# Target rows of a graph layer: a gather per edge replaced by one-hot matmuls on TensorE

## The chip, the core and the metric

The kernel runs on one core of a Trainium2 chip. The metric is the device time of one launch in microseconds (us), as the median of several runs without the profiler; lower is better. PE is TensorE, DVE is VectorE, ACT is ScalarE, POOL is GpSimd and SP is SyncE.

## The reference, cut to what matters

3125 nodes of 512 features and 50000 edges go through one layer with three parts: a message-passing network, a linear attention and a mixture of eight experts. The change concerns the messages. Per edge (`edge_dst` is the graph's `src`, which is sorted into target tiles by the kernel itself; `edge_src` its `dst`):

```python
pre = irrep_linear(x, W_pre0, b_pre0, W_pre1)
p0, p1 = split_irreps(pre)
pd0 = p0[edge_dst]
ip1 = jnp.einsum('eum,eum->eu', p1[edge_dst], p1[edge_src]) / 3.0
s0 = jnp.concatenate([pd0, pd0, ip1], axis=-1)
...
w = ssp(edge_attr @ W_f1) @ W_f2 * (ssp(s0 @ W_s1) @ W_s2)
w1, w2, w3, w4 = jnp.split(w, 4, axis=-1)
x0e, x1e = split_irreps(x[edge_src])
...
out = jax.ops.segment_sum(edge_feat, edge_dst, num_segments=old_x.shape[0])
```

So an edge needs two rows of its target (p0 folded into 32 hidden values, and p1, 384 values) and two of its source (p1 again, and the 512 values that make the message). `edge_feat` is made of `w`, the source's values and four edge numbers `sh`; the messages are summed per target.

## The kernel before, in words

The kernel has four stages. First, edges are sorted by target on the chip and their records (48 numbers) are scattered to memory in that order, while the node rows are computed; the rows go to two tables in memory, `rows_d` (target part, 32 + 384 values) and `rows_s` (source part, 384 + 512). Second comes the edge stage, from line 779, with which the change deals. Then the sums become new node rows and are routed, and last the experts run.

A target tile is 125 nodes, held as two halves of 63 and 62 (`TG`, `HT` = 64 rows of a half). A tile of edges is 128 edges whose targets lie in one half. Two edge tiles, one for each half, are a pair; eight pairs make up a target tile (`PER`), 25 target tiles make 200 pairs, and 12 more pairs (`NOV_MOST`) take what is over. Two pairs, four edge tiles, are a quad (`G`), with one record tile `rec`. The 212 pairs are 106 quads.

The order on PE, ACT, DVE and POOL is written out by hand (`tc.manual_schedule`, line 989): each engine runs its instructions in the order of the program text, and SP's transfers are put in order by the framework. A loop over steps `s` issues, in each step, the work of several pairs at different stages, and some of it only for a quad, every second step (`due`):

- `load` (SP): the record of a quad, 14 pairs ahead; `clear` (DVE) blanks places not in use, 10 ahead.
- `fetch` (POOL), `LEAD` = 9 pairs ahead: per edge tile one indirect transfer of the target rows `gd` (line 825) and one of the source rows `gx` (line 829).
- `products` (DVE, line 840), 7 or 6 pairs ahead: target p1 times source p1, into `prod`.
- `turn` (PE, line 847) 5 ahead: twelve transposes that also add the three components, into PSUM tile `ps_ip`; `turn2` copies it out on ACT (line 855).
- `hidden` (PE, lines 861, 866, 871), 4 ahead: the 32 hidden values of four tiles in one PSUM tile `ps_h`: the edge's own values turned, the target's values turned, and the inner products times `W_s1`.
- `softplus` (ACT, from line 879) and `softplus2` (DVE, line 891), 3 and 2 ahead; `which` (DVE, line 898): a one-hot of the edge's place in its half, 128 × 64 for each tile; `scaled` (ACT, line 913): the one-hot times each of the four edge numbers.
- `weigh`, 1 ahead: PE makes `wa` and `wb` (lines 924, 928), ACT copies `wa` to `wt` (line 930), DVE multiplies `wt` by `wb` (line 931).
- `feats` (DVE, lines 945, 949), 1 ahead: the message features `ft`.
- `gather_up` (PE, line 969): one-hots times features, summed in PSUM tile `ps_s` over the eight pairs; `kept` copies the sum to `acc`.

In a step of the kernel before, DVE runs clear, softplus2, which, products, then the multiplication of `weigh`, then `feats`. PE runs the weights, the hidden layer or the transposes, then the gather-up.

PSUM tiles before: `ps_ip` and `ps_h` one buffer each, `wa` and `wb` one each of 2 × 512 values, `ps_s` two.

Of the kernel before, what the change touches and what calls it, by code (L numbers as in the profile page):

```python
# [16 lines left out]
P = 128  # L17
EDGES = 50000
TG = 125
# [29 lines left out]
def gnn_mix_moe_kernel(ctx: ExitStack, tc: tile.TileContext, a: dict, out: bass.AP):  # L49
# [54 lines left out]

    rows_d = dram.tile([N, HID + 3 * MUL], F32, name="rows_d")
    rows_s = dram.tile([N, 3 * MUL + D], F32, name="rows_s")
# [33 lines left out]
    with ExitStack() as c1:  # L140
# [27 lines left out]
        for r in range(4):  # L168
# [5 lines left out]

        zero = tmp.tile([P, G * REC], F32, name="zero")
        nc.vector.memset(zero, 0.0)
        by_quad = recs.rearrange("(q p i) f -> p q (i f)", p=P, i=G)
        per = PER // PR
        cleared = [
            nc.gpsimd.dma_start(by_quad[:, qs, :], zero.unsqueeze(1).to_broadcast([P, n, G * REC]))  # L180
            for qs, n in (
                (slice(per - 1, NFIX // PR, per), NG), (slice(NFIX // PR, (NFIX + NOV_MOST) // PR), NOV_MOST // PR),
            )
        ]


# [592 lines left out]
    with ExitStack() as c2:  # L779
# [4 lines left out]
        ps_w = c2.enter_context(tc.tile_pool(name="ps_w", bufs=1, space=PSUM, reuse_waits="tile"))  # L784
        ps_o = c2.enter_context(tc.tile_pool(name="ps_o", bufs=2, space=PSUM, reuse_waits="tile"))

        w_s1c = w.tile([P, HID], F32, name="w_s1c")
# [12 lines left out]
        class Quad:  # L800
            pass

        quads = [Quad() for _ in range(NQ)]

# [13 lines left out]
        def fetch(Q, k):  # L818

            if k == 0:  # L820
                Q.gd = gat.tile([P, G, HID + 3 * MUL], F32, name="gd", bufs=3)
                Q.gx = gat.tile([P, G, 3 * MUL + D], F32, name="gx", bufs=5)
            reci = Q.rec.bitcast(I32)
            for i in (2 * k, 2 * k + 1):
                nc.gpsimd.indirect_dma_start(  # L825
                    out=Q.gd[:, (i + 2) % G, :], out_offset=None, in_=rows_d[:, :],
                    in_offset=bass.IndirectOffsetOnAxis(ap=reci[:, i, 5:6], axis=0),
                )
                nc.gpsimd.indirect_dma_start(  # L829
                    out=Q.gx[:, i, :], out_offset=None, in_=rows_s[:, :],  # L830
                    in_offset=bass.IndirectOffsetOnAxis(ap=reci[:, i, 4:5], axis=0),
                )

        def products(Q, k):

            if k == 0:
                Q.prod = work.tile([P, G, 3 * MUL], F32, name="prod")
            x = slice(2 * k, 2 * k + 2)
            d = slice(2 - 2 * k, 4 - 2 * k)
            nc.vector.tensor_mul(Q.prod[:, d, :], Q.gd[:, d, HID:], Q.gx[:, x, : 3 * MUL])  # L840

        def turn(Q):

            ps = ps_a.tile([P, G, P], F32, name="ps_ip")
            for i in range(G):
                for b in range(3):
                    nc.tensor.matmul(  # L847
                        ps[:, i, :], Q.prod[:, i, b * P : (b + 1) * P], ident, is_transpose=True,
                        start=(b == 0), stop=(b == 2),
                    )  # L850
            Q.ps_ip = ps
# [5 lines left out]
        def hidden(Q):  # L857

            Q.ps = ps_a.tile([P, 2, P], F32, name="ps_h")
            for i in range(G):  # L860
# [3 lines left out]
                )  # L864
            for i in range(G):
                nc.tensor.matmul(
                    Q.ps[i * HID : (i + 1) * HID, 1, :], Q.gd[:, i, :HID], ident,
                    start=True, stop=False, tile_position=(0, i * HID),
                )
            for i in range(G):  # L870
# [3 lines left out]
                )  # L874

        def softplus(Q, after=None):

            sp = work.tile([P, P], F32, name="sp")
            nc.scalar.activation(sp, Q.ps[:, 1, :], AF.Abs)
            if after is not None:  # L880
# [5 lines left out]
            Q.sp = sp  # L886
            Q.hT = work.tile([P, 2, P], F32, name="hT")
            nc.scalar.copy(Q.hT[:, 0, :], Q.ps[:, 0, :])

        def softplus2(Q):  # L890
            nc.vector.scalar_tensor_tensor(
                Q.hT[:, 1, :], Q.ps[:, 1, :], 0.0, Q.sp, op0=ALU.max, op1=ALU.add
            )

        def which(Q):

            Q.one = work.tile([P, G, HT], F32, name="one")
            nc.vector.tensor_tensor(
                Q.one, lane[:, :HT].unsqueeze(1).to_broadcast([P, G, HT]),
                Q.rec[:, :, 6:7].to_broadcast([P, G, HT]), op=ALU.is_equal,  # L900
            )

        class Pair:
            def __init__(self, Q, j):
                self.Q, self.j = Q, j
                self.tiles = (2 * j, 2 * j + 1)

        def scaled(R):

# [7 lines left out]
        def weigh(R):  # L917
# [4 lines left out]
            for k, i in enumerate(R.tiles):  # L922
                r = slice(i * HID, (i + 1) * HID)
                nc.tensor.matmul(wa[:, k, :], Q.hT[r, 0, :], w_f2[r, :], start=True, stop=True)  # L924
            for k, i in enumerate(R.tiles):
                i = (i + 2) % G
                r = slice(i * HID, (i + 1) * HID)
                nc.tensor.matmul(wb[:, k, :], Q.hT[r, 1, :], w_s2[r, :], start=True, stop=True)  # L928
            R.wt = work.tile([P, PR, D], F32, name="wt")
# [59 lines left out]
        with tc.manual_schedule(engines=steady):  # L989
# [21 lines left out]
            for s in range(-LEAD - 5, n_pairs + 1):  # L1011
                for Q in due(s + LEAD + 5):
                    q = quads.index(Q)
                    loaded = load(Q, recs[q * G * P : (q + 1) * G * P, :])
                    if q == 0:
                        for put in placed:
                            waits_for(loaded, put)
                for Q in due(s + LEAD + 1):
                    q = quads.index(Q)
                    clear(Q, real_slot[:, PR * q : PR * (q + 1), :])  # L1020
                for R in pair(s + LEAD):
                    fetch(R.Q, R.j)
                for Q in due(s + 2):
                    softplus2(Q)
                for Q in due(s + 3):
                    which(Q)
                for k in range(2):
                    for Q in due(s + 7 - k):
                        products(Q, k)
                for R in pair(s + 1):  # L1030
                    weigh(R)
                kept(s - 1)
                for Q in due(s + 3):
                    softplus(Q, table)
                for Q in due(s + 4):
                    hidden(Q)
                for Q in due(s + 5):
                    turn(Q)
# [6 lines left out]
                for R in pair(s):  # L1045
                    if s >= NFIX or s % PER == 0:
                        sums = ps_o.tile([P, D], F32, name="ps_s")
                    R.ps = sums
# [9 lines left out]
        with tc.If(some > NOV_MOST):  # L1058
            with tc.For_i(NOV_MOST // PR, (some + 1) // PR, 1) as i:
# [7 lines left out]
                clear(Q, real)  # L1067
                for k in range(2):
                    fetch(Q, k)
                for k in range(2):  # L1070
                    products(Q, k)
                turn(Q)
                turn2(Q)
                hidden(Q)
                softplus(Q)
                softplus2(Q)
                which(Q)
                for j in range(PR):
                    R = Pair(Q, j)
                    scaled(R)  # L1080
                    weigh(R)
                    feats(R)
                    ps = ps_o.tile([P, D], F32, name="ps_s")
                    gather_up(R, ps, True, True)
                    keep_sums(tile_of(whose[:, j : j + 1]), ps)

# [462 lines left out]
```

## Time and profile before

| what | us |
|---|---|
| median of three runs without profiler (2767.28 to 2779.3) | 2773.01 |
| the profiled execution's own time | 3138.92 |
| its span | 3137.2 |
| PE busy in the span (81%) | 2525.6 |
| DVE busy (54%) | 1684.5 |
| POOL busy (58%) | 1822.3 |
| ACT busy (37%) | 1162.2 |
| gathers of `gd`, 424 | 445.7 |
| gathers of `gx`, 424 | 483.7 |
| gather-up on PE (L969), 3392 instructions | 588.2 |

The profiled execution is longer than the runs without the profiler, so its own time is the base for sums that use its durations. The page of a profile cuts the span into 40 slices of 78 us and shows the busy share of each engine in tenths:

```profile
PE   2576493882788888888888888888679999999998
DVE  7988330211667777776777767777842222222222
POOL 0688666664656666666666666664345555555552
PEclk9688696995888889888898988889889999999999
```

PEclk is the clock that PE was granted, in tenths of full speed. The edge stage is the even stretch from about the eleventh slice to the twenty-eighth. Line numbers (L825) are those of the kernel before. "A <- B" means that A waited for B, or that A's output is made from B; "issue" is a wait that the profile gives no cause for. A matmul of 32-bit numbers shows as two instructions, so that counts of PE are double there.

### The profile page before, as it was taken

The page shows a single profiled execution, that of the slowest core. Times are in us where ns is not written, and L with a number is a line of the kernel's source. Part 1 is how long each engine was busy: PE and PEld are TensorE (multiplying, and loading weights), DVE is VectorE, ACT ScalarE, POOL GpSimd, SP SyncE. Part 2 cuts the span into 40 slices and gives each one's busy share as a digit, 9 for nine tenths or more (in the row PEclk, how much of TensorE's full clock was granted, in tenths as well). Part 3 has the DMA queues.
Part 4 walks back from the last instruction along what each step waited for, and adds up shares of the span by engine and source line. Part 5 has one row for each costly group of instructions (what it writes and reads, how often), then busy time and mean ns, then how long its engine had stood idle before and what let it go on. Part 6 is the DMA issues. An engine that isn't in the chain of part 4 may idle for free. (4 is left out here: it accounts for less than half of the span.)

```text
span 3137.2 us, 46186 instructions
## 1 busy us (share of the span) xinstructions
PE 2525.6 (81%) x16716; PEld 1592.3 (51%) x16716; DVE 1684.5 (54%) x3084; ACT 1162.2 (37%) x3261; POOL 1822.3 (58%) x1741
## 2 busy tenths in 40 slices
PE   2576493882788888888888888888679999999998
PEld 2343242551333444343444434343568888888887
DVE  7988330211667777776777767777842222222222
ACT  1244240110555555555565555556411111111111
POOL 0688666664656666666666666664345555555552
PEclk9688696995888889888898988889889999999999
DMA  7777202555666667676676766676662442785552
GB/s 257 245 262 247 70 24 91 163 175 162 202 204 207 204 197 221 201 212 200 206 218 207 213 204 201 198 206 146 214 247 66 147 149 68 265 291 171 176 171 103
DMA packets 200361, 581.25 MB, mean 185 GB/s; under 512 B 55130, under 2 KB 80400, under 8 KB 189374
## 3 DMA queue, kind: packets, MB, share of 16 engines
q0 software_dynamic: 126176, 455.15, 46.9%
q1 hardware_dynamic: 50718, 83.23, 7.7%
q10 hardware_dynamic: 23232, 39.84, 4.0%
q8 instruction: 135, 2.21, 0.3%
q14 instruction: 100, 0.82, 0.1%
HBM read 635.69 MB, written 112.28 MB: 238 GB/s over the span
## 5 line engine op out<-in xcount | busy, mean ns | idle before, releaser
L829 POOL DMA_INDIRECT gx<-rows_s,rec x424 | 483.7, 1141 | 262.1 <-DVE ft L949 138.5
L969 PE MATMUL ps_s<-ft,ones 128*64 128x256 f32 (+1 forms) x3392 | 588.2, 481 | 17.8 <-issue 15.2
L825 POOL DMA_INDIRECT gd<-rows_d,rec x424 | 445.7, 1051 | 266.5 <-issue 108.1
L459 POOL DMA_INDIRECT recs<-again,at_i x391 | 425.8, 1089 | 236.0 <-issue 111.6
L931 DVE TENSOR_TENSOR wt<-wt,wb 128x1024 f32<-128x1024 f32 x212 | 258.4, 1219 | 382.4 <-ACT wt L930 236.9
L913 ACT ACTIVATE ones<-one,rec 128x64 f32<-128x64 f32 x1696 | 428.1, 339 | 0.0
L1411 PE MATMUL ps_f<-h,we 128*128 128x128 f32 x3392 | 406.7, 278 | 17.9 <-ACT h L1424 15.2
L969 PEld LDWEIGHTS ps_s<-ft,ones 128*64 128x64 f32 x3392 | 254.8, 149 | 301.5 <-issue 238.0
L1411 PEld LDWEIGHTS ps_f<-h,we 128*128 128x128 f32 x3392 | 388.6, 192 | 32.1 <-ACT h L1424 24.9
L949 DVE TENSOR_TENSOR ft<-wt,gx 128x768 f32<-128x768 f32 x424 | 386.0, 952 | 0.0
L930 ACT COPY wt<-wa 128x1024 f32<-128x1024 f32 x212 | 214.3, 1011 | 424.6 <-PE wb L928 207.0
L1426 DVE TENSOR_SCALAR h<-ps_f,bias 128x128 f32<-128x128 f32 x318 | 108.3, 350 | 482.1 <-PE ps_f L1411 450.7
L1338 POOL DMA_INDIRECT we<-w_rows,w_at x212 | 214.7, 1013 | 259.5 <-PE ps_y L1442 101.0
L1424 ACT ACTIVATE h<-ps_f,bias 128x128 f32<-128x128 f32 x318 | 110.7, 366 | 672.9 <-PE ps_f L1411 607.1
L928 PE MATMUL wb<-w_s,hT 32*128 32x512 f32 x848 | 270.8, 655 | 11.2 <-issue 8.3
L924 PE MATMUL wa<-w_f,hT 32*128 32x512 f32 x848 | 252.9, 650 | 7.5 <-issue 5.7
L840 DVE TENSOR_TENSOR prod<-gd,gx 128x768 f32<-128x768 f32 x212 | 202.3, 954 | 33.9 <-DMA gx<-rows_s,rec 21.5
L1411 PEld LDWEIGHTS ps_f<-xt,we 128*128 128x128 f32 x1696 | 199.2, 193 | 26.0 <-issue 24.9
L847 PEld LDWEIGHTS ps_ip<-ident,prod 128*128 128x128 f32 x1272 | 140.4, 143 | 122.4 <-issue 122.3
L1411 PE MATMUL ps_f<-xt,we 128*128 128x128 f32 x1696 | 199.6, 276 | 0.7 <-ACT xt L1359 0.7
L847 PE MATMUL ps_ip<-ident,prod 128*128 128x128 f32 x1272 | 166.7, 281 | 41.4 <-DVE prod L840 33.5
L1442 PE MATMUL ps_y<-we,h 128*128 128x512 f32 x424 | 196.1, 605 | 0.8 <-ACT h L1424 0.7
(337 smaller groups left out, 3114.0 us busy)
## 6 DMA issues: line engine op xcount, KB each, us to landing
w_rows<-in_Wh ACTq DMA_DIRECT2D x24, 1024.0 KB
rows_s<-r SPq DMA_DIRECT2D x24, 448.0 KB
rec<-recs SPq DMA_DIRECT2D x106, 96.0 KB
lined<-rec SPq DMA_DIRECT2D x14, 672.0 KB
again<-lined POOLq DMA_DIRECT2D x14, 672.0 KB
w_rows<-in_Wo ACTq DMA_DIRECT2D x8, 1024.0 KB
gd<-rows_d,rec POOLq DMA_INDIRECT x424
gx<-rows_s,rec POOLq DMA_INDIRECT x424
```

Of the source, the lines that this page charges most:

```text
L459: put = nc.gpsimd.indirect_dma_start(out=recs[:, :], out_offset=bass.IndirectOffsetOnAxis(ap=at_i[:m, t : t + 1], axis=0), in_=again[c][:m ...
L825: nc.gpsimd.indirect_dma_start(out=Q.gd[:, (i + 2) % G, :], out_offset=None, in_=rows_d[:, :], in_offset=bass.IndirectOffsetOnAxis(ap=reci ...
L829: nc.gpsimd.indirect_dma_start(out=Q.gx[:, i, :], out_offset=None, in_=rows_s[:, :], in_offset=bass.IndirectOffsetOnAxis(ap=reci[:, i, 4:5 ...
L847: nc.tensor.matmul(ps[:, i, :], Q.prod[:, i, b * P : (b + 1) * P], ident, is_transpose=True, start=(b == 0), stop=(b == 2),)
L913: nc.scalar.activation(R.ones[:, k, c, :], R.Q.one[:, i, :], AF.Copy, scale=R.Q.rec[:, i, c : c + 1])
L924: nc.tensor.matmul(wa[:, k, :], Q.hT[r, 0, :], w_f2[r, :], start=True, stop=True)
L928: nc.tensor.matmul(wb[:, k, :], Q.hT[r, 1, :], w_s2[r, :], start=True, stop=True)
L931: nc.vector.tensor_mul(R.wt, R.wt, wb)
L949: nc.vector.tensor_mul(R.ft[:, k, MUL : 7 * MUL].rearrange("p (b c u) -> p b c u", b=2, c=3), w[:, k, :, 1, :].unsqueeze(2).to_broadcast([ ...
L969: nc.tensor.matmul(to, R.ones[:, k, m, :], what, start=(first and m == 0), stop=(last and m == 3), tile_position=(0, k * HT),)
L1338: nc.gpsimd.indirect_dma_start(out=dst, out_offset=None, in_=src, in_offset=bass.IndirectOffsetOnAxis(ap=at[:, j : j + 1], axis=0), bounds ...
L1411: nc.tensor.matmul(pss[f], ws[l][:, k, f * P : (f + 1) * P], h[:, k, :], start=(k == 0), stop=(k == 3))
```

## The change

The target rows of an edge tile are no longer gathered by edge. The rows of a half target tile (64 rows) are loaded once for all eight pairs into a tile `own` by plain transfers on SP (`targets`), and PE spreads them over the edges: the one-hot of an edge tile is turned (`over`: two transposes a quad, copied to `oneT` by ACT), and `own_rows` multiplies it with `own`, so that each edge gets its target's row, in PSUM tile `gd`. `products` reads `gd` there, once a pair. `hidden` takes the target's hidden values from `own` and `oneT` in the same way. `which` moves from 3 pairs ahead to 10 ahead, with six buffers.

`ps_one`, `ps_ip` and `ps_h` share one PSUM buffer (tag "turned"); `ps_s` has one buffer[...]. `hidden2` copies the hidden layer's PSUM tile out on ACT, and the softplus works on the copy.

The order in a step changes too: fetch, weigh, kept, softplus2, products, clear, which, over, softplus, hidden, own_rows, turn, feats, turn2, scaled, gather_up. Two more rows of zeros stand at the end of `rows_d`, so that the last half tile can be loaded whole.

```diff
-    rows_d = dram.tile([N, HID + 3 * MUL], F32, name="rows_d")
+    rows_d = dram.tile([N + 2, HID + 3 * MUL], F32, name="rows_d")
...
+        for part in (slice(0, HID), slice(HID, HID + 3 * MUL)):
+            nc.gpsimd.dma_start(rows_d[N:, part], zero[:2, : part.stop - part.start])
...
-        ps_o = c2.enter_context(tc.tile_pool(name="ps_o", bufs=2, space=PSUM, reuse_waits="tile"))
...
         def fetch(Q, k):
...
             for i in (2 * k, 2 * k + 1):
                 nc.gpsimd.indirect_dma_start(
-                    out=Q.gd[:, (i + 2) % G, :], out_offset=None, in_=rows_d[:, :],
-                    in_offset=bass.IndirectOffsetOnAxis(ap=reci[:, i, 5:6], axis=0),
-                )
-                nc.gpsimd.indirect_dma_start(
                     out=Q.gx[:, i, :], out_offset=None, in_=rows_s[:, :],
...
+        def targets(b):
+            own = gat.tile([P, HID + 3 * MUL], F32, name="own", bufs=4)
+            for k in range(PR):
+                nc.sync.dma_start(own[k * HT : (k + 1) * HT, :], rows_d[bass.ds(b * TG + k * (HT - 1), HT), :])
+            return own
+
+        def which(Q):
+            Q.one = work.tile([P, G, HT], F32, name="one", bufs=6)
...
+        def over(Q):
+            ps = ps_a.tile([P, G, P], F32, name="ps_one", tag="turned")
+            for j in range(PR):
+                nc.tensor.transpose(
+                    ps[:, j, :], Q.one[:, PR * j : PR * (j + 1), :].rearrange("p k t -> p (k t)"), ident
+                )
+            Q.oneT = work.tile([P, PR, P], F32, name="oneT", bufs=4)
+            nc.scalar.copy(Q.oneT, ps[:, :PR, :])
+
+        def own_rows(R):
+            R.gd = ps_a.tile([P, PR, D], F32, name="gd")
+            for k in range(PR):
+                h = slice(k * HT, (k + 1) * HT)
+                nc.tensor.matmul(
+                    R.gd[:, k, : 3 * MUL], R.Q.oneT[h, R.j, :], R.own[h, HID:], start=True, stop=True,
+                    tile_position=(k * HT, 0),
+                )
...
-            nc.vector.tensor_mul(Q.prod[:, d, :], Q.gd[:, d, HID:], Q.gx[:, x, : 3 * MUL])
+            nc.vector.tensor_mul(Q.prod[:, d, :], R.gd[:, :, : 3 * MUL], Q.gx[:, x, : 3 * MUL])
...
             for i in range(G):
+                R = Q.pairs[1 - i // PR]
+                h = slice(i % PR * HT, (i % PR + 1) * HT)
                 nc.tensor.matmul(
-                    Q.ps[i * HID : (i + 1) * HID, 1, :], Q.gd[:, i, :HID], ident,
-                    start=True, stop=False, tile_position=(0, i * HID),
+                    Q.ps[i * HID : (i + 1) * HID, 1, :], R.own[h, :HID], Q.oneT[h, R.j, :],
+                    start=True, stop=False, tile_position=(i % PR * HT, i * HID),
                 )
...
+        def hidden2(Q):
+            Q.hT = work.tile([P, 2, P], F32, name="hT", bufs=3)
+            nc.scalar.copy(Q.hT, Q.ps[:, :2, :])
...
+                for R in pair(s + LEAD + 3):
...
+                        R.own = targets(at // PER)
...
+                for R in pair(s + LEAD):
+                    fetch(R.Q, R.j)
+
+                for R in pair(s + 1):
+                    weigh(R)
+                kept(s - 1)
+                for Q in due(s + 2):
+                    softplus2(Q)
+                for R in pair(s + 7):
+                    products(R)
                 for Q in due(s + LEAD + 1):
                     q = quads.index(Q)
                     clear(Q, real_slot[:, PR * q : PR * (q + 1), :])
-                for R in pair(s + LEAD):
-                    fetch(R.Q, R.j)
-                for Q in due(s + 2):
-                    softplus2(Q)
-                for Q in due(s + 3):
                     which(Q)
-                for k in range(2):
-                    for Q in due(s + 7 - k):
-                        products(Q, k)
-                for R in pair(s + 1):
-                    weigh(R)
-                kept(s - 1)
+                for Q in due(s + LEAD):
+                    over(Q)
                 for Q in due(s + 3):
                     softplus(Q, table)
                 for Q in due(s + 4):
                     hidden(Q)
+                    hidden2(Q)
+                for R in pair(s + 8):
+                    own_rows(R)
                 for Q in due(s + 5):
                     turn(Q)
                 for R in pair(s + 1):
...
                     if s >= NFIX or s % PER == 0:
-                        sums = ps_o.tile([P, D], F32, name="ps_s")
+                        sums = ps_a.tile([P, D], F32, name="ps_s")
```

The branch for more than 12 pairs over is changed alike; with these inputs it is not entered. `weigh` issues the same four matmuls in another order (wa, wb, wa, wb).

## Prediction

> **What bounds the kernel now.** I read the granted clock and the totals first, then busy time by stage, then the timeline of one quad (four edge tiles, two pairs) inside the edge stage, then the waits there. By stage (columns: stretch, length, busy time and count of PE, PE's weight loads, DVE, ACT, POOL, then granted clock, DMA share, GB/s):
>
> ```profile
> 742.70:797.00 54.30, 15.38 (x124) 10.51 (x124) 13.08 (x20) 9.40 (x29) 39.24 (x39) 0.53 0.77 234
> 797.00:2213.60 1416.60, 1209.73 (x8788) 569.34 (x8780) 1028.75 (x1369) 788.04 (x2435) 890.17 (x810) 0.89 0.68 200
> ...
> 2280.00:3137.20 857.20, 818.62 (x5824) 698.54 (x5824) 228.31 (x577) 139.55 (x373) 427.24 (x423) 0.99 0.49 167
> ```
>
> The edge stage is 1416.6 us of 3137.2 us for 106 quads: 13.4 us each. The rest of the profiled time of 3138.9 us is 1722.3 us. The expert stage (from 2280) has PE busy nearly all along; the change doesn't touch it.
>
> The quads are not alike: the transposes L847, one burst per quad, start at 1052.09, 1061.58 and 1079.42 us, 9.49 and then 17.84 us apart. In the short quad the engines look like this (start, duration, engine, line):
>
> ```profile
> 1057.03 1.01 ACT L930 COPY wt<-wa 128x1024 f32<-128x1024 f32 x1 [0.32 <-PE wb L928]
> 1057.08 0.28 DVE L891 SCALAR_TENSOR_TENSOR hT<-ps_h,sp 128x128 f32<-128x128 f32 x1
> 1057.28 0.95 DVE L840 TENSOR_TENSOR prod<-gd,gx 128x768 f32<-128x768 f32 x1
> 1057.41 0.16 PEld L861 LDWEIGHTS ps_h<-ident,rec 128*32 128x32 f32 x8 [1.25 <-DVE rec L813]
> ...
> 1058.14 1.22 DVE L931 TENSOR_TENSOR wt<-wt,wb 128x1024 f32<-128x1024 f32 x1
> ...
> 1058.21 2.37 PE L969 MATMUL ps_s<-ft,ones 128*64 128x512 f32 x16
> ...
> 1060.51 0.70 PE L924 MATMUL wa<-w_f,hT 32*128 32x512 f32 x2
> ...
> 1061.58 1.53 PE L847 MATMUL ps_ip<-ident,prod 128*128 128x128 f32 x12
> ...
> 1063.05 2.37 PE L969 MATMUL ps_s<-ft,ones 128*64 128x512 f32 x16
> ```
>
> From start to next start on PE: hidden layer (L861, 866, 871) 0.80, gather-up (L969) 2.30 per pair, weights (L924/928) 1.07 per pair, transposes 1.46; per quad 0.80 + 2×2.30 + 2×1.07 + 1.46 = 9.0 us with hardly a gap. DVE's ops in the same spacing make 9.7 us: per pair 0.86 (L840) + 1.25 (L931) + 0.61 + 1.74, per quad 0.78 more. POOL's gathers follow each other by 0.95 + 0.30 = 1.25 us at best, eight a quad: 10.0 us; with their mean durations it is 4×(1.05 + 1.14 + 0.60) = 11.2. Three engines sit near 10 us. In the long quads PE issues a few matmuls every 1.4 us and waits for nothing that is named:
>
> ```profile
> PEld ps_s L969 <- issue: 201.9, 630, 1.9
> DVE wt L931 <- ACT wt L930: 187.5, 76, 5.9
> ACT wt L930 <- PE wb L928: 173.2, 95, 4.9
> POOL gx L829 <- DVE ft L949: 116.8, 39, 5.1
> POOL gd L825 <- PE ps_h L866: 84.4, 33, 7.8
> ```
>
> (waiter, releaser, total, times, longest, from 1000 to 2200 us). POOL's own waits are for buffers, so POOL runs ahead. The reader should take two things from it: POOL isn't alone at the limit, and L931 follows ACT's copy, which follows PE, in every pair.
>
> The run without the profiler takes 2773 us, 366 less. The expert stage can't give that; the unnamed PE waits can. I hold them for a cost of profiling, an inference. POOL's floor of 10.0 us lets the edge stage shrink by 1416.6 − 1060 = 357 at most; some of the 366 may sit before 742, where the waits called remote and issue add up to some 156 us (ACT r L709 101.0 and DVE y L734 54.8). Halfway, 80, the edge stage before is 1131 us unprofiled, 10.7 a quad.
>
> [...] after PE's idle from 458.85 to 461.60 (2.75 us) the clock was 0.50 from 463 to 466; after one of 2.37 us at 468 it stayed up. [...] four 32-row matmuls of L924 and L928 start within 0.02 us.
>
> **The change, part by part.**
>
> Removed: 424 gd gathers. POOL falls from eight gathers to four, 5.0 to 5.6 us a quad; the DMA engines lose 424 × 213 KB = 90 of 581 MB and get some 8 MB of direct loads back. Neither was alone at the limit, so this by itself is worth at most 11.2 − 9.7 us a quad, and what is late next are DVE and PE.
>
> Added on ACT: copies of oneT and of two hidden columns of tiles, each 256 wide; between 0.245 (128 wide) and 0.586 (512 wide) that is 0.36 each, less the 0.245 of L888: +0.5 us on 7.4 busy a quad. Covered. DVE: the product reads gd from PSUM instead; L931 reads PSUM at 1.22 us for 1024 and L840 SBUF at 0.95 for 768, the same rate, so 0. SP: `own`, two loads per eight pairs, asked for at pair s+12 and used at s+8, four steps ahead; its queue only holds record loads that wait for `scaled` of pair s−1. Covered; for the last twelve pairs, where each has its own load behind `hidden` of an earlier pair, up to 1.5 us each, not counted. The zero rows and the larger memset stand at the program's start under DVE and POOL work: 0.
>
> Added on PE: `over`, 2 of the 12-transpose kind, 0.24 us a quad; `own_rows`, per pair two matmuls of 384 columns over 64 rows in different row groups: from 1.07 us for 512 columns side by side, 0.80; in series it would be 1.60. The hidden layer's rows of `own` swap one set of four for another: 0. PE's work is then 9.0 + 0.24 + 1.60 = 10.9 us.
>
> The new wait decides. `gd` has one buffer. In step s, own_rows(s+8) overwrites what products(s+7) reads, and products was moved behind weigh(s+1) on DVE, whose L931 waits for ACT's copy, which waits for PE's weights of the same step. Behind own_rows on PE stand the transposes and the gather-up, and behind them the next step's weights. So the step becomes a ring through three engines, once a pair. Walk it from the start of wa at 0: ACT starts at 1.18 (1055.85 to 1057.03) and takes 1.01; DVE starts 0.03 later, 2.22; L931 holds it 1.25, to 3.47; the product 0.95, to 4.42; PE takes the signal 0.05 later, 4.47 (L861 after L891 shows that lag); own_rows to 5.27. Odd step: transposes 1.46, gather-up 2.30: 9.03. Even step: softplus2 is ahead of the product, +0.20; no transposes: 4.67 + 0.80 + 2.30 = 7.77. `over` and the hidden layer fall into PE's wait, so they cost nothing. `turn` needs the shared bank from the oneT copy, done at about 2.6: hidden too. Sum 16.8 us a quad.
>
> PE then idles from 1.4 to 4.5 in the odd step and from 2.0 to 4.7 in the even one: 3.0 and 2.7 us, just the size after which the clock halved above. Bounds: never, 0; always down to a mean of 0.8, then the 9.7 us of PE in the ring cost 9.7 × 0.25 = 2.4. I take about one fall a quad, 3 us at half speed with some two thirds of it on PE work: +1.0. Quad 17.8.
>
> Sum: 106 × 17.8 = 1887; twelve additions of late sums (L977, 0.68) now lie in the ring, +8; the fill from 742.7 to 797 is paced by ten pairs of gathers and loses half, −25. Edge and fill change by 1887 + 8 − 25 − 1416.6 = +453, so 3138.9 becomes about 3592 on the profile's footing. Of the 1722.3 us outside, 80 don't occur without the profiler (0 to 156): 3512. I say 3510, 27% over the median. That the unnamed PE waits vanish in the edge stage needs no subtraction here: the ring replaces that stage.
>
> **The rivals.**
> - The ring isn't closed (gd is free when PE comes, PE only gets more work): quad 10.9 + 0.4 gap (9.49 less PE's 9.07 now) = 11.3, edge 1198, total 1722 + 1198 − 25 − 80 = 2815. For it: PE is the busiest engine. [...]
> - Not slower: POOL paces the unprofiled kernel at 11.2 us a quad, and PE at 10.9 keeps under it. Gain 106 × 0.3 + 25 = 57: 2716. Place: the gather stream; it decides only if PE's stall per quad stays under 0.3 us. Against: a stall of 5.7 is worked out above.
> - The clock stays down at 0.6 in most of the stage: 9.7 × 0.67 = 6.5 more, quad 23.3, edge 2470 + 8: total 1722 + 2478 − 25 − 80 = 4095. For it: every gap is near the size. Against: own_rows, transposes, gather-up and weights are 5 to 6 us of dense work between gaps.
> - own_rows in series: +1.6 a quad, 3680, inside the range.
>
> **How the numbers follow.** Forecast with its own range 0.80, clock down 0.08, ring open 0.07, not slower 0.05. Low end: no fall of the clock and 156 us taken off, 1722.3 − 156 + 1781 + 8 − 25 = 3330, 3325 stated. High end: 2.4 us a quad for the clock and nothing taken off, 1722 + 2035 − 17 = 3740. Half a per cent is about what a measurement of this kernel can tell from no change: faster 0.04, within it 0.02, slower 0.94.
>
> **What would show it.** DVE's product waits for nothing, but PE's own_rows waits for DVE's product some 2.5 to 3 us, twice a quad; L931 again behind ACT's copy; POOL half idle, waiting for feats; quads 17 to 18 us apart; clock in the stage below 0.95; own_rows 0.8 us from start to next start. I am wrong if PE runs through own_rows without a wait, or if the expert stage changes.

## The result, and the profile after

The changed kernel takes 3724.9 us (3722.76 to 3726.74, four runs) against 2773.31 us for the kernel before in the same comparison: a ratio of 1.3431 (95% interval 1.3401 to 1.3461). It is slower by a third. The forecast was 3510 us with a range from 3325 to 3740.

By stage, from the answer that lists stretches of the span (length, busy time and count of PE, PE's weight loads, DVE, ACT and POOL, then granted clock, DMA share, GB/s):

```profile
900.00:2700.00 1800.00, 1332.26 (x8272) 599.48 (x8272) 853.01 (x1143) 710.90 (x2130) 332.68 (x352) 0.79 0.31 98
...
2800.00:3723.00 923.00, 860.23 (x6232) 740.08 (x6232) 305.28 (x743) 191.28 (x455) 454.73 (x474) 0.97 0.52 176
```

No engine is full in the edge stage: PE is busy for 74% of it, DVE for 47%, POOL for 18%, and PE's clock is 0.79. The page's slices show the same over the whole span:

```profile
PE   2667991777777777777777777777776799999998
POOL 0887777211212111211112121212102455555553
PEclk9888995778777777877787777778778899999999
```

The gather-up (now line 997) starts first at 688.3 us and last at 2831.2: the stage has become 2142.9 us long. What lies outside it, 3724.9 − 2142.9 = 1582 us, is what it was before (1584, by the first experiment). So all of the loss is in the edge stage. The waits there (waiter, releaser, total us, times, longest):

```profile
POOL gx L825 <- DVE ft L977: 1593.5, 101, 18.0
ACT wt L958 <- PE wb L956: 826.2, 210, 8.0
DVE wt L959 <- PE ps_h L905: 619.4, 103, 7.5
...
PE gd L860 <- DVE prod L872: 542.0, 203, 6.0
DVE wt L959 <- ACT wt L958: 503.9, 108, 6.2
```

PE waits at `own_rows` (L860) for DVE's product in 203 of 212 pairs. DVE waits at the weights' multiplication (L959, before L931) for ACT in the odd steps. In the even ones the name beside it is the hidden layer, but L959 doesn't read `ps_h`, and it starts 0.03 us after ACT's copy ends in both. ACT waits for PE's weights. Each of the three waits for the one before it in a circle. POOL only waits for a buffer of `gx` to come free.

The timeline of one turn and a half (start, duration, engine, line, tile; in brackets the idle time before it and what ended it):

```profile
1504.21 1.65 PE L860 MATMUL gd<-own,oneT 64*128 64x384 f32 x4 [2.38 <-DVE prod L872]
...
1505.79 4.54 PE L997 MATMUL ps_s<-ft,ones 128*64 128x512 f32 x16
...
1516.35 2.82 PE L879 MATMUL ps_ip<-ident,prod 128*128 128x128 f32 x12
...
1531.51 0.69 PE L955 MATMUL wa<-w_f,hT 32*128 32x512 f32 x1
...
1532.70 1.01 ACT L958 COPY wt<-wa 128x1024 f32<-128x1024 f32 x1 [6.01 <-PE wb L956]
...
1533.74 1.22 DVE L959 TENSOR_TENSOR wt<-wt,wb 128x1024 f32<-128x1024 f32 x1 [4.05 <-ACT wt L958]
...
1534.88 0.95 DVE L872 TENSOR_TENSOR prod<-gd,gx 128x768 f32<-128x768 f32 x1
...
1535.98 0.92 PE L860 MATMUL gd<-own,oneT 64*128 64x384 f32 x4 [2.96 <-DVE prod L872]
...
1536.83 1.53 PE L879 MATMUL ps_ip<-ident,prod 128*128 128x128 f32 x12
...
1538.29 2.37 PE L997 MATMUL ps_s<-ft,ones 128*64 128x512 f32 x16
```

From 1531.51 on this is an odd step at full clock, and it is the predicted ring. Counted from the start of `wa` at 1531.51: ACT starts after 1.19, DVE after 2.23, the product after 3.37, own_rows after 4.47, and the next `wa` (1540.59) after 9.08 us, with 9.03 worked out ahead. The three lines at the top are the same work at half clock: own_rows takes 1.65 instead of 0.92, the gather-up 4.54 instead of 2.37, the transposes 2.82 instead of 1.53. Transposes of successive quads start 20.48 us apart (1495.86, 1516.35, 1536.83). The sum had 17.8.

The granted clock has only two values here, 0.50 and 1.00, and the stretches between its changes, over two quads, are these (columns as in the table by stage, the clock third from the end):

```profile
1503.54:1510.37 6.83, 6.16 (x24) 2.33 (x24) 3.62 (x6) 0.96 (x5) 2.30 (x3) 0.50 0.18 38
1510.37:1513.78 3.41, 1.43 (x10) 0.43 (x10) 1.25 (x2) 2.21 (x5) 1.49 (x2) 1.00 0.90 294
1513.78:1520.61 6.83, 5.84 (x20) 3.48 (x22) 3.18 (x4) 1.40 (x5) 0.00 (x0) 0.50 0.23 86
1520.61:1527.44 6.83, 4.45 (x50) 1.78 (x46) 3.04 (x6) 4.40 (x15) 0.00 (x0) 1.00 0.17 46
1527.44:1530.85 3.41, 3.41 (x14) 1.42 (x14) 2.25 (x3) 0.00 (x0) 0.89 (x1) 0.50 0.00 0
1530.85:1544.50 13.65, 8.98 (x82) 4.17 (x78) 6.10 (x8) 7.36 (x22) 2.90 (x4) 1.00 0.46 143
```

At 1544.50 the next fall begins, 40.96 us after the first one here, and the pattern starts again.

### The profile page after: what moved, and what is told of

Read it like the earlier page. It is cut to its first block, busy times and chain, and to the rows that moved or that the text cites. A ratio compares the mean times of both kernels' runs of the same rounds, so it can differ in the third digit from the quotient of the medians.

```text
span 3723.0 us, 47635 instructions
## 1 busy us (share of the span) xinstructions
PE 2859.6 (77%) x17776; PEld 1719.9 (46%) x17776; DVE 1683.4 (45%) x3084; ACT 1232.4 (33%) x3367; POOL 1291.0 (35%) x1319
## 5 line engine op out<-in xcount | busy, mean ns | idle before, releaser
L825 POOL DMA_INDIRECT gx<-rows_s,rec x424 | 401.2, 946 | 1702.7 <-DVE ft L977 1593.5
L959 DVE TENSOR_TENSOR wt<-wt,wb 128x1024 f32<-128x1024 f32 x212 | 258.9, 1221 | 1127.3 <-PE ps_h L905 619.4
L997 PE MATMUL ps_s<-ft,ones 128*64 128x256 f32 (+1 forms) x3392 | 736.8, 594 | 18.7 <-DVE acc L1005 18.7
L860 PE MATMUL gd<-own,oneT 64*128 64x384 f32 x848 | 277.1, 733 | 561.7 <-DVE prod L872 542.0
L997 PEld LDWEIGHTS ps_s<-ft,ones 128*64 128x64 f32 x3392 | 298.6, 184 | 458.5 <-issue 422.4
L860 PEld LDWEIGHTS gd<-own,oneT 64*128 64x128 f32 x848 | 89.2, 245 | 614.3 <-issue 333.1
L955 PE MATMUL wa<-w_f,hT 32*128 32x512 f32 x848 | 243.1, 646 | 0.0
L956 PE MATMUL wb<-w_s,hT 32*128 32x512 f32 x848 | 242.9, 646 | 0.0
L879 PEld LDWEIGHTS ps_ip<-ident,prod 128*128 128x128 f32 x1272 | 198.1, 183 | 85.8 <-issue 85.3
L879 PE MATMUL ps_ip<-ident,prod 128*128 128x128 f32 x1272 | 232.0, 352 | 0.0
L887 ACT COPY ip<-ps_ip 128x512 f32<-128x512 f32 x106 | 62.1, 586 | 466.2 <-PE ps_ip L879 466.2
```

The costliest lines, as they stand in the source:

```text
L825: nc.gpsimd.indirect_dma_start(out=Q.gx[:, i, :], out_offset=None, in_=rows_s[:, :], in_offset=bass.IndirectOffsetOnAxis(ap=reci[:, i, 4:5 ...
L860: nc.tensor.matmul(R.gd[:, k, : 3 * MUL], R.Q.oneT[h, R.j, :], R.own[h, HID:], start=True, stop=True, tile_position=(k * HT, 0),)
L879: nc.tensor.matmul(ps[:, i, :], Q.prod[:, i, b * P : (b + 1) * P], ident, is_transpose=True, start=(b == 0), stop=(b == 2),)
L956: nc.tensor.matmul(wb[:, k, :], Q.hT[q, 1, :], w_s2[q, :], start=True, stop=True)
L959: nc.vector.tensor_mul(R.wt, R.wt, wb)
L997: nc.tensor.matmul(to, R.ones[:, k, m, :], what, start=(first and m == 0), stop=(last and m == 3), tile_position=(0, k * HT),)
```

## The experiments

Three questions were open: is it the ring, and the ring alone, that holds PE up; how much is the clock's; and what paced the kernel before, on which the worth of the whole change hangs. The runs were made on four chips. On two of them (e0 to e3; e10 and e11) the kernel before takes 2765 to 2769 us, as on the chip of the result above, on the other two (e4 to e7; e8 and e9) 3198 to 3200, so times are compared within one chip, and between the two kinds of chip only by the length of the edge stage (first to last start of the gather-up) or by the distance between quads. The changed kernel's 3724.9 us goes with 2773 us for the kernel before, 0.3% above the 2765 of e0 to e3, and is set beside them.

### The kernel before, profiled again (e0)

The same kernel, to see whether the profiler or something else made the first profile 366 us longer than the median.

> The kernel before, profiled once more. The profile of before took 3139 us against a median of 2773, the profile of the changed kernel 3724.8 against 3724.9. Theory P (profiling slows the kernel before, by PE's unnamed waits): again about 3140, with quads 9.5 and 17.9 us apart. Rival (that execution was an odd one, and profiling costs nothing): 2770 to 2785, quads about 11.2 us apart (2773 less the 1554 us that the changed kernel spends outside 106 quads of 20.48, over 106, is 11.5 with the fill in it).

It took 2759.36 us under the profiler, and the median of nine runs without it on that chip was 2764.84. The profiler costs nothing that can be seen. The edge stage as a stretch, and POOL's timeline in it:

```profile
691.80:1866.90 1175.10, 1024.39 (x8783) 514.18 (x8780) 1032.87 (x1367) 783.26 (x2426) 882.41 (x813) 0.96 0.81 242
```

```profile
1205.96 0.96 POOL L825 DMA_INDIRECT gd<-rows_d,rec  x1 [0.30 <-issue]
1207.23 0.95 POOL L829 DMA_INDIRECT gx<-rows_s,rec  x1 [0.30 <-DVE wt L931]
1208.48 1.17 POOL L825 DMA_INDIRECT gd<-rows_d,rec  x1 [0.30 <-issue]
```

POOL never rests longer than the 0.30 us between two gathers in this stretch, and DVE's product waits for gathered rows (gx, 73.0 us in 112 waits from 1000 to 1700 us): the stream of gathers is the limit. 1175.1 / 106 = 11.09 us a quad, against the 11.2 that the prediction had from the mean durations. The waits of PE's matmuls that had no name in the first profile (hidden layer, L866 and L861 <- issue, 45.8 and 39.3 us in the stage) are gone. The weight loads' unnamed waits, which the prediction showed, are nearly as long for the time (L969, 109.3 us in 405 waits from 1000 to 1700 us), but none is longer than 0.6 us, where the longest was 1.9.

### The product ahead of the weights on DVE (e1), own_rows last on PE (e2)

The ring can be opened at either end. e1 moves one instruction on DVE, e2 one group on PE, both from the changed kernel:

```diff
 e1
+                for R in pair(s + 7):
+                    products(R)
                 for R in pair(s + 1):
                     weigh(R)
...
-                for R in pair(s + 7):
-                    products(R)
 e2
-                for R in pair(s + 8):
-                    own_rows(R)
                 for Q in due(s + 5):
                     turn(Q)
...
                     gather_up(
...
+                for R in pair(s + 8):
+                    own_rows(R)
```

> The changed kernel with one edit: on DVE, products of pair s+7 ahead of the multiplication of weigh of pair s+1. Theory A (the ring PE, ACT, DVE, PE through the single gd buffer sets the step): the ring is open, gd is free when PE comes to own_rows, quads of 11.3 us paced by PE, clock in the stage near 1, 1554 + 106 x 11.3 = 2752, range 2700 to 2850. Rival B (PE's added work and a clock that the new mix of matmuls pulls down set it): nothing of PE's work changes, 3600 to 3725. Rival C (the shared PSUM bank of the three turned tiles sets it): unchanged too, 3700.

> The changed kernel with one edit: on PE, own_rows of pair s+8 stands after the gather-up of the step instead of before it; DVE's order stays. Theory A: transposes and gather-up fill PE's wait, own_rows comes up at 4.8 to 5.1 us of the odd step, where the product is done at 4.4, so it waits little: quads of 11.3 to 12 us, 2750 to 2830. In the even step hidden 0.8 + gather-up 2.3 end at 4.2, the product at 4.6, so 0.4 us of wait is left. Rival B and C: 3600 to 3725.

e1 took 2892.22 us, 1.047 times the kernel before (1.0453 to 1.0488), e2 2937.55, 1.0635 times (1.0617 to 1.0652). Moving one DVE instruction, with every transfer, every matmul and every buffer left as it is, gave back 833 of the 952 us; the clock in the stage rose to 0.99. That is the ring, together with the low clock that its gaps bring (e3 parts the two). Both stayed above what was expected of them, for two reasons. PE's own work is 11.4 us a quad, not 10.9 (worked out under e6). And another wait comes out in each. In e1 (timeline):

```profile
1306.85 0.95 DVE L872 TENSOR_TENSOR prod<-gd,gx 128x768 f32<-128x768 f32 x1
...
1307.86 0.92 PE L860 MATMUL gd<-own,oneT 64*128 64x384 f32 x4 [0.82 <-DVE prod L872]
```

The product still starts only when DVE is done with the features of the pair before, so PE waits 0.82 us a quad at own_rows: 12.2 us from quad to quad. In e2 that wait is nearly gone (0.17), but the transposes, no longer delayed by own_rows, wait 1.02 us a quad for ACT's copy of `oneT`, which has to leave the shared PSUM buffer first: 12.7 us.

### Both orders (e6)

The two edits together, to see whether PE then gets down to its own work.

> The edits of e1 and e2 together: products first on DVE, own_rows after the gather-up on PE. e1's quad was 12.2 us with 0.82 of wait at own_rows left in the odd step. Theory A (PE's work alone is left, 12.2 - 0.8 = 11.4 us a quad): 2892 - 106 x 0.8 = 2807, range 2790 to 2830. Rival (something else than own_rows' wait holds e1, so moving it gives nothing): 2880 to 2940.

3055.44 us on a chip where the kernel before takes 3200.34 (ratio 0.9548, 0.9505 to 0.9591). By its quads it missed: 12.4 us, every fourth 13.0, where 11.4 was looked for; hardly better than e2. PE's longest wait in sum, over the run:

```profile
PE ps_ip L879 <- ACT oneT L853: 106.2, 103, 2.6
```

The wait at own_rows is gone and that for the shared buffer stays, 106.2 / 103 = 1.0 us a quad. ACT copies `wt` first and then `oneT`, and the transposes stand behind both. The prediction held the wait for it, its "shared bank", to be hidden. It was, behind own_rows' wait in the ring; in the open it costs 1.0 us a quad. Take each run's waits off its quads, and the same is left three times: 12.22 − 0.82 in e1, 12.66 − 1.02 − 0.17 in e2, 12.42 − 1.03 here, 11.4 to 11.5 us. That is PE's work; none of the three runs got down to it.

### PE kept busy in its gaps (e3), in one of the two (e7)

To weigh the clock by itself, e3 leaves the ring closed and fills PE's two gaps of a quad with matmuls into columns of the shared tile that nothing reads:

```diff
         ps = ps_a.tile([P, G, P], F32, name="ps_one", tag="turned")
+            for _ in range(5):
+                nc.tensor.matmul(ps[:, PR:, :], ident, w_s2[:, : PR * P], start=True, stop=True)
...
         Q.ps = ps_a.tile([P, G, P], F32, name="ps_h", tag="turned")
+            for _ in range(4):
+                nc.tensor.matmul(Q.ps[:, 2:, :], ident, w_s2[:, : 2 * P], start=True, stop=True)
```

e7 has only the first of them, in the odd step.

> The changed kernel with added matmuls whose results nobody reads: five of 128x256 ahead of the turned one-hots and four ahead of the hidden layer, in unused columns of the same PSUM tile, some 2.4 and 1.9 us at full clock, inside PE's wait of 3.0 and 2.7 us. The ring is as it was. Theory A with the clock as multiplier (16.8 us a quad at full clock, 3.7 lost by the half clock after each idle): the clock stays up, 16.8 to 17.2 us a quad, 1554 + 106 x 17 = 3356, range 3320 to 3420. Rival (the clock is no part of it and PE's own work is): slower than 3725 by up to 106 x 4.3 = 456 us.

> As e3 but the unread matmuls only in the odd step (five of them), none ahead of the hidden layer: one of two idles per quad is filled. The changed kernel's quads are all 20.48 us[...]. Theory A[...]: one idle of 2.7 us is left, quads between 16.8 and 20.48[...]; range 3350 to 3560. Rival (each idle costs half of 3.7 us[...]): 18.65 us, 1554 + 106 x 18.65 = 3531.

e3 took 3372.3 us (ratio 1.2204, 1.2184 to 1.2225), in the middle of what was expected. Adding nine matmuls a quad made the kernel 353 us faster than the changed kernel. The stretch in the stage:

```profile
1000.00:1700.00 700.00, 649.71 (x4660) 361.49 (x4656) 404.37 (x540) 342.00 (x1010) 158.77 (x168) 1.00 0.38 120
```

The clock is 1.00, and quads are 16.81 us apart (1007.17, 1023.98, 1040.79): the ring without its clock is the 16.8 that the prediction's walk gave. The rest, 20.48 − 16.81 = 3.67 us a quad, is the clock's.

e7 took 3592.44 us, above the 3350 to 3560 expected, but on a chip where the kernel before takes 3200.34 (ratio 1.1228, 1.1178 to 1.1278), while the expected times were for 2765. By its quads it lies inside the 16.8 to 20.48 expected, short of the rival's 18.65: they are 16.8, 16.8, 16.8, 19.8 and 18.5 us apart in turn (in some turns one of the 16.8 is missing), 17.8 on the mean. Half of the clock's loss didn't come out, and the distance is not fixed as the changed kernel's 20.48 is. One gap filled leaves 1.0 of the 3.7 us: PE is slow twice in five quads (own_rows takes 1.65 us at 1048.25 and 1.55 at 1068.07, and 0.92 between), and the mean clock from 1000 to 1700 us is 0.94. Two falls of 6.83 and 3.41 us, an estimate, would give that: 1 − 0.5 × 10.24 / 88.7.

### No gather of target rows at all (e4)

The kernel before, with its 424 gathers of `gd` left out and one constant tile in their place. The inner products and the target's hidden values are then not those of the reference. It shows the most that taking these gathers from POOL could bring.

```diff
+        gd1 = w.tile([P, G, HID + 3 * MUL], F32, name="gd1")
+        nc.vector.memset(gd1, 0.5)
...
-                Q.gd = gat.tile([P, G, HID + 3 * MUL], F32, name="gd", bufs=3)
+                Q.gd = gd1
...
-                nc.gpsimd.indirect_dma_start(
-                    out=Q.gd[:, (i + 2) % G, :], out_offset=None, in_=rows_d[:, :],
...
```

> The kernel before with the 424 gathers of target rows left out: gd is one constant tile, so the inner products and the target's hidden values are not the reference's; everything else is done. Theory D (POOL's gathers, back to back at 11.1 us a quad, pace the kernel before, and DVE stands right behind at 9.7): 2765 - 106 x (11.1 - 9.8) = 2627, range 2600 to 2660. Rival E (POOL is not what paces it; PE at 9.1 or the chain of PE, ACT and DVE in a step is): 2740 to 2770.

It took 2733.36 us where the kernel before takes 3200.34 (ratio 0.853, 0.8494 to 0.8567). The expected 2600 to 2660 were for a chip with 2765, and e4 did not run on one, so the stage has to decide. It is 1023.6 us (793.9 to 1817.5), 151 less than in e0 where 138 were expected, and its quads are 9.7 us apart throughout, which is DVE's own work: the products of one order start at 1200.31, 1210.00 and 1219.70, and DVE follows itself without a gap. So 11.09 − 9.7 = 1.4 us a quad, some 147 us of the kernel (11.09 × 106 less 9.7 × 106), was there to be had on the faster kind of chip, and all of it only for a version that costs PE less than 0.7 us a quad on top of its 9.0. PE's work in the changed kernel, 10.9 us as predicted and 11.4 as found, takes nearly all of it or more back before any wait. On the slower kind of chip leaving the gathers out is worth 467 us, and there even e6, which spreads every row, is faster than the kernel before. e4 takes away POOL's issuing and the transfers at once; which of the two sets the pace of the gathers it doesn't tell.

### Half gathered, half spread (e5 and e9, e8 and e11, e10)

POOL has time for six gathers a quad (eight took 11.09 us in e0, so six make 8.3, an estimate), and PE for one of the two own_rows (0.84 us each in e1, 1302.38 to 1303.22). e5 gathers the target rows of the first pair of a quad and spreads those of the second, with the product ahead of the weights as in e1. Some buffers of `own`, `one` and `hT` are given up for it. Its core, from the changed kernel:

```diff
+                if k == 0:
+                    nc.gpsimd.indirect_dma_start(
+                        out=Q.gd[:, i, :], out_offset=None, in_=rows_d[:N, :],
...
         def own_rows(R):
+            if R.j == 0:
+                return
...
+            gd = Q.gd[:, :, HID:] if k == 0 else R.gd[:, :, : 3 * MUL]
```

e8 also issues `over` ahead of `weigh`, so that ACT copies `oneT` before `wt`:

```diff
+                for Q in due(s + LEAD):
+                    over(Q)
                 for R in pair(s + 1):
                     weigh(R)
...
-                for Q in due(s + LEAD):
-                    over(Q)
```

e9 and e11 are e5 and e8 once more on another chip, and e10 is e8 with the hidden layer's matmuls of 64 rows put last instead of in the middle.

> products first as in e1, and target rows gathered by POOL for the first pair of each quad and spread by PE for the second only. POOL six gathers, 6 x 1.4 = 8.4 us; PE 9.1 + 0.3 (hidden layer in two tilings) + 0.3 (one turned one-hot) + 0.85 (one own_rows) = 10.5; DVE 9.7. own_rows comes every second step, so gd is free long before. Theory A and D together: 10.5 to 10.7 us a quad against 11.1, 2765 - 106 x 0.5 = 2712, range 2690 to 2740, faster than both kernels. Rival (mixing the two ways makes new waits, as on gx transfers or the deeper own and oneT buffers cut here): 2765 to 2850.

> As e5 (products first on DVE; the target rows of the first pair of each quad gathered, those of the second spread by PE), but the turning of the one-hot and its copy to oneT stand ahead of the weights in the step, so that ACT makes the oneT copy before the copy of wt, and the transposes no longer wait for it through the shared PSUM bank. Theory (the bank's wait of 0.2 to 0.3 us a quad was what kept e5 off PE's work): quads of 10.5 to 10.8 us, edge stage 1115 to 1150 us against 1177 in e5, 30 to 60 us less than e5 on the same chip; on a chip on which the kernel before takes 2765, 2690 to 2740, a ratio of 0.97 to 0.99. Rival (the wait was slack, and PE's hidden layer in three tilings and its gather-up fill the turn anyway): within 10 us of e5. Rival (the oneT copy ahead of wt delays the wt copy by 0.36 us, and DVE's products with it): up to 20 us slower than e5.

> e5 once more, beside e8 on the same chip. Theory: edge stage 1170 to 1180 us as in the first run of it. If this chip runs the kernel before at about 2765 us, then the ratio to it is 0.99 to 1.01 (quads of 11.0 against 11.1); if it runs it at about 3200, the ratio is again 0.90, because half gathered has fewer transfers and hardly meets the unnamed PE waits of that chip.

> As e8, but in the hidden layer the two matmuls of 64 rows that take the target's hidden values from own stand last instead of between the matmuls of 128 rows[...]. Theory (the change of tiling is what made the hidden layer 1.26 us where before it took 0.80 and in the changed kernel 1.07): hidden layer 1.0 to 1.15 us, quads of 10.35 to 10.5 us against 10.57, 10 to 25 us less than e8. Rival (two matmuls that share PE where four could is what costs it, not the change): hidden layer 1.2 to 1.3 us, within 8 us of e8.

> e8 once more, beside e10 on the same chip. Expected: edge stage 1150 to 1156 us as in its first run. On a chip on which the kernel before takes about 2765 (edge stage 1175), that makes 2735 to 2750, a ratio of 0.99 to 0.995; on one that takes 3200 before, again 0.896.

| run | us | before, same chip | ratio (95% interval) | edge stage, us |
|---|---|---|---|---|
| e5 | 2897.37 | 3200.34 | 0.9042 (0.9010 to 0.9073) | 1177 |
| e9 (as e5) | 2899.06 | 3197.6 | 0.9048 (0.9013 to 0.9083) | 1180 |
| e8 | 2872.46 | 3197.6 | 0.8964 (0.8928 to 0.8999) | 1153 |
| e11 (as e8) | 2724.54 | 2768.84 | 0.9836 (0.9817 to 0.9855) | 1145 |
| e10 | 2717.3 | 2768.84 | 0.9807 (0.9788 to 0.9826) | 1138 |

e5 fell short of its 10.5 to 10.7 us a quad (10.8 to 11.2): the transposes waited for the `oneT` copy, 0.2 to 0.3 us a quad, and its stage, 1177 us, is no shorter than e0's 1175. e8 takes that wait away and is 27 us faster than e9 on the same chip, just under the 30 expected. On a chip that runs the kernel before at 2769 us, e11 and e10 are faster than the kernel before, by 1.6 and 1.9% (a small gain, but its intervals keep clear of 1), and so than both kernels; e11 did a little better than the 2735 to 2750 expected of it. In both, PE runs with hardly a wait, at 10.57 and 10.45 us a quad.

e10 changed less than hoped, 7 us where 10 to 25 were expected. Its hidden layer (timeline: L902 to the gather-up, 1.13 us against 1.25 in e11):

```profile
1310.20 0.43 PE L902 MATMUL ps_h<-ident,rec 128*32 128x128 f32 x8
...
1310.99 0.41 PE L919 MATMUL ps_h<-oneT,own 64*32 64x128 f32 x4
1311.33 2.37 PE L1011 MATMUL ps_s<-ft,ones 128*64 128x512 f32 x16
```

Two matmuls of 64 rows still take 0.34 us, where four of 128 rows took 0.27 in the kernel before (0.80 / 3). The change of shape in the middle costs 0.12 us, the smaller part of the 0.45 by which e11's hidden layer is longer than the kernel before's.

## Why the prediction came out as it did, point by point

**What bounds the kernel now.** That POOL, DVE and PE stand near one another at 11.2, 9.7 and 9.0 us a quad was right, and the gathers at their mean durations are what paces: 11.09 in e0, and DVE's 9.7 as soon as those of the target rows are gone (e4). "POOL runs ahead" holds for the first profile and not for e0. The reading of the unnamed PE waits as a cost of profiling was wrong: e0 has none of those of PE's matmuls under the same profiler, and chips on which the kernel before takes 3200 us without a profiler exist. The first profile, 3139 us, fits one of that kind: its gather-up starts 105 us later than in e0 (797.1 against 691.8) and 34 us more lie behind it, nearly what parts e8 and e11, the same kernel on the two kinds of chip (110 and 37). The error was in drawing a base for the unprofiled kernel from an inference (an edge stage of 1131 us; it is 1175). It hardly moved the forecast, because the ring replaces the whole stage, and outside it 80 us were taken off where e0 has 138 less (1584 against 1722): the sum held 1722 − 80 − 25 = 1617, and 1582 was measured.

**The new wait.** Right, and to 0.05 us in the odd step. Undoing the order on DVE (e1), nothing else, gave back 833 us; filling PE's gaps without opening the ring (e3) left the quads at 16.81 us. The rival "ring isn't closed" was put at 2815; opened, it is 2892. A quad is 12.2 us instead of 11.3: PE's work is 11.4 us instead of 10.9, and PE's gap 0.8 instead of 0.4, because the product waits behind the features. That is 98 us in 106 quads, and what lies outside the stage came out smaller.

**The clock.** This is the term that was mis-sized. The prediction took 1.0 us a quad, for one fall with 3 us at half speed, two thirds of it on PE's work, and gave 2.4 as the most. Measured: 20.48 − 16.81 = 3.7, over the bound. All three parts of the 1.0 were too small. Two quads hold three falls; they last 6.83, 6.83 and 3.41 us, 5.7 on the mean; and PE runs matmuls for 6.16, 5.84 and 3.41 us of them, nine tenths. Half of these 15.4 us is 7.7 in two quads, close to the 7.3 that were lost. The step that failed in the bound is "always down to a mean of 0.8, then the 9.7 us of PE in the ring cost 9.7 × 0.25". The mean was right, 0.79, which is half speed for 42% of the time. But that isn't spread evenly over PE's idle and busy time, as 9.7 × 0.25 takes it: PE is busy for 74% of the stage, and for nine tenths of the half-speed time. The instructions show it: own_rows after a gap took 1.65, 1.65, 0.98 and 0.92 us in four steps running (1504.21, 1514.77, 1526.72, 1535.98), and the gather-up or the transposes behind it are slow in the first three. The third fall came only 0.7 us after own_rows had started. The prediction's argument against a low clock, 5 to 6 us of dense work between gaps, didn't prevent the falls and makes each of them expensive; but the clock did come back, and the rival with a mean of 0.6 didn't happen.

**The sum.** The clock's +2.68 us × 106 = +284 us too little; the stage measured from first to last gather-up covers about 1.4 quads less than 106, −28; the twelve additions of late sums, +8, didn't show beside that; and −35 outside the stage. From 1895 + 1617 = 3512, stated as 3510: 3512 + 284 − 28 − 8 − 35 = 3725, which is what was measured. That the time fell inside the range is in part luck: the upper end held the clock's bound and nothing taken off outside, the one too low and the other too high, which nearly made up for each other.

**PE's added work.** own_rows came out at 0.85 us side by side (1535.98 to 1536.83), with 0.80 predicted, so the rival of 1.60 in series falls. `over`, 0.24 predicted from start to next start, shows as 0.44 from start to end in e1 (1306.60); nothing follows it closely enough to tell more. The hidden layer, "swap one set of four for another: 0", was wrong: in e1 it takes 1.07 us (1301.31 to 1302.38) against 0.80. A set with 64 rows stands between two with 128 there; e10 and e11, which differ in where that set stands, put a change of shape in the middle at about 0.1 us (1.13 against 1.25). In the changed kernel `over` and the hidden layer fall into PE's wait and cost nothing, as predicted.

**ACT, DVE, SP and the shared buffer.** DVE's product took 0.95 us from PSUM as from SBUF. ACT's copies of 256 columns took 0.38 us, with 0.36 predicted. The wait for the shared buffer is hidden in the changed kernel, and e2 and e6 show its price once own_rows doesn't stand there: 1.0 us a quad.

**Not tried.** The changed kernel with two buffers of `gd`. Whether PSUM has room for the second, no trace or run here shows. That it would open the ring without a change of order stays an argument; e1 shows that the order alone opens most of it.

## What to carry to other kernels

When a tile with one buffer links two engines, write down the instructions that stand between its reader and its writer on each queue, and walk round: a consumer placed behind an instruction that waits for the producer's engine closes a ring. Here the order of two lines on DVE cost 833 us, the low clock included, and the gathers that the change takes away had some 147 us to give. When such a ring leaves PE idle for 2.4 to 3 us again and again, estimate the low clock by its falls: how many there are, how long each lasts (here 3.4 or 6.8 us) and how much of that lies on PE's work (here nine tenths). The mean clock times the busy time gave too little. And before moving work from a pacing engine, measure the most it can bring by leaving it out (here 1.4 us a quad) and compare it with what the other engine has free (0.7 to DVE's limit, 2.1 to that of the gathers): the half of the change that fits is what was faster, by 1.6 to 1.9% here and by 10% on the slower kind of chip.

## What the runs showed of the hardware that was not expected

- **A loop in step with the changes of the clock.** Every stretch of one clock in the table of the result lasts 3.41, 6.83 or 13.65 us: one, two or four times 3.413. All stretches that end inside the trace of the changed kernel (347) or of the kernel before (135) are whole multiples of 3.413 us. Twelve times 3.413 are 40.96 us, the two quads of the table. The changed kernel's transposes start every 20.48 us, six times 3.413, to 0.01 us through most of the stage, though hidden layers are alternately 22.50 and 18.46 us apart (1500.70, 1523.20, 1541.66). With all gaps filled the distance is 16.81, no multiple. With one gap filled (e7) there is no fixed distance, but its five quads of 16.8, 16.8, 16.8, 19.8 and 18.5 us make 88.7, 26 times 3.413. So the loop keeps step with this length in two kernels. That it is pulled there by the clock's changes is an inference; no run tests it apart.
- **The length of a gap alone doesn't decide.** PE's idle times of 2.38, 2.97 and 2.38 us before own_rows (1504.21, 1514.77, 1526.72) went with half clock, and one of 2.96 (1535.98) didn't. In the kernel before, the prediction had found half clock after 2.75 us and full clock after 2.37; here 2.38 was enough twice. How a gap lies against the clock's steps of 3.41 us might explain the difference; that isn't shown.
- **Two kinds of chip.** The kernel before takes 2765 to 2769 us on two chips and 3198 to 3200 on two others; the version of e8 and e11 takes 2725 and 2872. Comparing its two profiles, 110 us lie before the first gather-up (681.0 and 790.7), 8 in the edge stage and 37 behind it. In the kernel before, the edge stage grew as well, by 240 us, if the first profile is of the slower kind (1175 in e0, 1415 there, with PE's long waits that have no name). The half-gathered version hardly showed that. What makes those chips slow is open.
